# Two query passes for the last batch, deeper expert buffers and other GpSimd costs in an attention and expert kernel

## The chip, the cores and the metric

The kernel runs on one core of a Trainium2 chip. The metric is the device time of one launch in microseconds. The kernel before takes 2341.13 us, the median of 3 runs (2332.34 to 2346.16).

## The reference

The input is 4 batches of 2048 tokens with 256 features. The layer has two halves, each wrapped in a layer norm before and a layer norm after, with a residual:

```python
x = x + layernorm(attention(layernorm(x)))
x = x + layernorm(ffn(layernorm(x)))
```

The attention has 16 heads of 16 features. Queries and keys are projected to one number per token and head, `zq` and `zk`, and a key counts by how near its number is to the query's:

```python
out[i] = sum_j max(0, 1 - abs(zq[i] - zk[j]) / bandwidth[h]) * v[j] / T      # T = 2048
```

The reference computes this with a sort and prefix sums; the value is that of the sum over all 2048 x 2048 pairs of a head. The second half is a mixture of experts: softmax over 64 experts, the best 8 of each token with their weights normalised, at most 128 tokens for an expert (counted in the order of all 8192 tokens, the rest are dropped), each expert a gated layer 256 to 128 to 256, and a shared expert 256 to 512 to 256 that every token passes, scaled by a sigmoid gate:

```python
w, idx = top_k(softmax(x @ gate_w), 8);  w = w / w.sum()
pos = running count of the token within its expert       # pos >= 128: dropped
y = sum over kept (token, expert): w * (silu(g) * u) @ down[e]
out = y + (silu(G) * U) @ shared_down * sigmoid(x @ shared_gate_w)
```

Everything is float32.

## The kernel before

**The loop.** The attention is 1024 units, 256 for each batch: two groups of 8 heads (`NG`), two halves of a group (`p`), 16 tiles of 128 keys (`NT`), 4 heads (`j`). In a unit all 2048 queries of a head (`qb`, broadcast to 128 partitions by `load_q`) meet 128 keys. `score(t)` makes the weights: `abs(q - k)` of 128x2048, mostly on ACT (L1558, Abs with the key as bias), and on DVE in two instructions (L1553, L1555) when the counter `spare` has saved up enough DVE time; then DVE's min and subtract (L1562). `product(t)` multiplies with the values: four matmuls (L1588) of 512 queries on 32 columns of PE, one for each query chunk c, and chunk c is that of the unit c earlier, so the four matmuls of a step have four heads `j` and lie on four column tiles. The sums stay in four PSUM banks (`pa0` to `pa3`) over a group and are brought out by `evict` (L1572), then stored in `cx_d`. The weights live in 13 big tiles of 128x2048 (`NBIG`), and smaller work in 10 slots (`NSLOT`).

**The background.** After each unit `bg.step()` lets the class `Background` issue other work from one list in order of priority. A task has an engine, a cost in units, dependencies, buffers that it takes (`get`) and gives back (`put`), and an optional `lat`, from which the wait of its successors is worked out. `CAP` limits the cost per engine and step, and a task is issued when its dependencies are old enough and its buffers free. Nothing else sets the order in which the engines receive this work. `flush(tasks)` issues the named tasks and all that they depend on at once, and `drain()` empties the list after the loop, with one unit of cost per step. GpSimd's gathers were entered at cost 1.3 and its scatters at 1.9, both with `lat=5`.

The background work of batch b is `prepare(b)` (norm and projections, one batch ahead), and `finish(b)`, put in the list eight units into the next batch: `front(c)` for each of 4 chunks of 512 tokens (transposes, residual, norm, router logits L543), `tail()` (softmax, best 8, codes of the chosen experts transposed into `scT`), `first` (rounds of MAX8 and MATCH_REPLACE, L713 and L715, which choose the earliest tokens of each expert), and `shared(c)`, the shared expert (L573, L587, L589, L602, L607, store to `y_d` at L619, collected in `stored[b]`). For batches 0 and 1 it then enters `all_experts`: 64 experts, each with a load of weights on SP, a gather of up to 128 rows on POOL (L1041), transposes and matmuls (L1047, L1051, L1061), Silu and products, and a scatter with addition to `y_d` (L1066). Four row sets and four weight halves allow for some overlap; expert e waits for the scatter of e-4, its weights for the gather of e-2.

**The tail.** After the loop `bg.flush(tabs + chain)` issues what routing work is left, and the last batch follows: `front_last` (all four chunks), eight rounds of `first`, `merge` and `ranking`, and 15 items, which serve the experts' places that are still free for tokens of batches 2 and 3 (gather L1217, matmuls, two scatters L1258 where an item holds two experts). A scatter waits for `stored[2]`, the shared expert of batch 2. The rest of the list, among it the shared expert of batch 2, goes between `front_last` with its merging and the items:

```python
mine = bg.q
bg.q = mine + rest
ys = stored[2]
```

Then come `shared_last` (the shared expert of the last batch, L911 to L931, kept on chip), and `final` for 16 chunks of 512 tokens (load of `y_d` L1281, add L1288, statistics L1292, power on POOL L1298, norm L1307, an accumulating DMA to the output on POOL L1321). Those of batches 2 and 3 wait for the last item's scatter. A branch for overflowing experts follows and is not taken here.

Of the kernel before, what the change touches and what calls it, by code (L numbers as in the profile page):

```python
# [25 lines left out]
class Background:  # L26
# [8 lines left out]
    def __init__(self, make):  # L35
        self.make = make
        self.free = {}
        self.q = []
        self.t = 0
        self.debt = dict.fromkeys(self.CAP, 0.0)  # L40
        self.spent = dict.fromkeys(self.CAP, 0.0)
        self.alone = False
# [27 lines left out]
    def emit(self, k):  # L70
        for key, r in k.get.items():
            tag, _ = self.free[r].pop(0)
            k.env[key] = self.make(tag)
            k.env["tag", key] = (r, tag)
# [66 lines left out]
def sandwich_kernel(ctx: ExitStack, tc: tile.TileContext, x_in, wqT, bq, wkT, bk, wvT, bv, wprojT, log_bw,  # L141
                    gate_w, sgate_w, sgu_w, sd_w, egu_w, ed_w, out):
    nc = tc.nc
# [36 lines left out]
    cx_d = [dram.tile([NG, P, T], F32, name=f"cx_d{b}") for b in range(B - 1)]  # L180
# [5 lines left out]
    ysh_d = dram.tile([T, F], F32, name="ysh_d")  # L186
# [28 lines left out]
    NS = NT // 2 * P  # L215
    scT = const.tile([P, NS + CAP], F32, name="scT")
# [9 lines left out]
    with ExitStack() as ph:  # L226
# [30 lines left out]
        NES, ess = 4, []  # L257
        bg = Background(make)
        bg.free["slot"] = [(f"s{i}", 0) for i in range(NSLOT)]
# [196 lines left out]
        def finish(b, after=()):  # L456
# [5 lines left out]
            xfree = []  # L462
            def front(c):
# [93 lines left out]
                a = bg.add("act", 0.25, gate, [a])  # L557
                gts = bg.add("dve", 0.1, lambda gt=gt: nc.vector.tensor_scalar(gt, gt, 0.5, 0.5, ALU.mult, ALU.add), [a])
                ready[c] = (done, gt, gts)

            def shared(c):
# [32 lines left out]
                for i2 in range(2):  # L594
# [15 lines left out]
                    if i2 == 0:  # L610
# [8 lines left out]
                free_ys = bg.add("sp", 1.0, lambda ys=ys, r0=r0: nc.sync.dma_start(yrows(r0, CH, 0),  # L619
                                                                                   chunkview(env[ys])),  # L620
                                 yy, put=[] if b == NE else [ys], env=env)
                stored[b].append(free_ys)
                if b == NE:
                    bg.add("sp", 1.0, lambda ys=ys, c=c: nc.sync.dma_start(rows(ysh_d, c * CT, CH), chunkview(env[ys])),
                           [free_ys], put=[ys], env=env)

            def tail():


                lgv = lambda: env["lg"].rearrange("p (n e) -> p n e", e=E + 1)[:, :, :E]  # L630
                mkv = lambda: env["lg"][:, :NT * E].rearrange("p (n e) -> p n e", e=E)
                prv = lambda: env["pr"][:, :NT * E].rearrange("p (n e) -> p n e", e=E)
                mx = t8 = ts_ = None
                t0 = b * NT
                wide = lambda a: a.unsqueeze(2).to_broadcast([P, NT, E])

                def most():
                    nonlocal mx, t8, ts_
                    mx = small.tile([P, NT], F32, tag="mx", name=f"mx_{b}")
                    t8 = small.tile([P, NT, TOPK], F32, tag="t8", name=f"t8_{b}")  # L640
                    ts_ = small.tile([P, NT], F32, tag="ts", name=f"ts_{b}")
# [13 lines left out]
                for i in range(0, NT, 4):  # L655
                    a = bg.add("dve", 0.55, lambda i=i: top(i), [a])
                for i in range(0, NT, 4):
                    a = bg.add("dve", 0.78, lambda i=i: rep(i), [a])

                def sums():  # L660
# [6 lines left out]
                tabs.append(bg.add("sp", 1.0, lambda: nc.sync.dma_start(tabrows(b * T, NT)[:, :, F:TW], prv()), [a],  # L667
                                   put=["pr"], env=env))
                a = bg.add("dve", 1.2, lambda: nc.vector.scalar_tensor_tensor(
                    out=mkv(), in0=mkv(), scalar=0.0, in1=wide(code[:, t0:t0 + NT]), op0=ALU.is_lt, op1=ALU.mult), [a])  # L670
                ev = []
                for r in range(NT // 8):
                    pk = ("psc", r)

                    def tr(r=r, pk=pk):
                        for i in range(4):
                            t = r * 8 + 2 * i
                            nc.tensor.transpose(env[pk][:, i * P:(i + 1) * P],
                                                mkv()[:, t:t + 2, :].rearrange("p a e -> p (a e)"), ident)
                    t_ = bg.add("pe", 0.58, tr, [a], get={pk: "bank"}, put=["lg"] if r == NT // 8 - 1 else [], env=env)  # L680
                    ev.append(bg.add("dve", 0.68, lambda r=r, pk=pk: nc.vector.tensor_copy(
                        scT[:, r * BK:(r + 1) * BK], env[pk]), [t_] + chain[-1:], put=[pk], env=env))
                return ev

            for c in range(NCH):
                front(c)
            if b < NE:
                for c in range(NCH):
                    shared(c)
            a = tail()  # L690
            if b < NE - 1:
                a = first(a, CAP, NS + CAP)
                a = bg.add("dve", 0.2, lambda: nc.vector.tensor_copy(scT[:, NS:], codes), [a])
            elif b == NE - 1:
                a = early(first(a, CAP, NS + CAP), stored[0] + stored[1])
            else:
                a = keep(a, 0)
                a = first([a], LP, NS)
                a = bg.add("dve", 0.2, lambda: nc.vector.tensor_copy(scT[:, NS:NS + LP], codes[:, :LP]), [a])
            chain.append(a)  # L700
            if b == NE:
                for c in range(NCH):
                    shared(c)

        def keep(ev, i):
            return bg.add("sp", 1.0, lambda: nc.sync.dma_start(ck_d[i][:, :], scT[:, :NS]), ev)

        def first(ev, n, w):

            a = ev[-1]  # L710
            for r in range(n // 8):
                c8 = codes[:, r * 8:(r + 1) * 8]
                a = bg.add("dve", 1.25, lambda c8=c8: nc.vector.max(out=c8, in_=scT[:, :w]), ev + [a])  # L713
                if r < n // 8 - 1:
                    a = bg.add("dve", 1.25, lambda c8=c8: nc.vector.match_replace(  # L715
                        out=scT[:, :w], in_to_replace=c8, in_values=scT[:, :w], imm_value=0.0), [a])
# [1073 lines left out]
```

## Time and profile before

| | us |
|---|---|
| median of 3 runs | 2341.13 |
| profiled execution | 2339.91 |
| its span | 2338.0 |
| until the loop starts | 76.7 |
| loop, batch 0 / 1 / 2 / 3 | 473.6 / 489.7 / 500.0 / 505.2 |
| tail, to the first item gather | 82.8 |
| tail, to the first scatter | 76.5 |
| tail, to the last scatter | 68.8 |
| tail, to the end | 64.7 |

The profiled execution is the one whose trace is read here; its span is what the trace covers. The granted clock of TensorE had a mean of 0.954. The stretches are cut at the first unit of each batch and at GpSimd's first item gather, first scatter and last scatter. Engines are PE (matmul), PEld (weight load), DVE, ACT, POOL (GpSimd) and SP (DMA issue). A row of the groups reads: line, engine, operation, output<-inputs, shapes, count | busy time and mean ns of one | idle time of the engine just before, with what ended it. A row of a timeline reads: start, duration, engine, line, operation, and in brackets the idle time before it and its releaser.

### The profile page before, as it was taken

Reading aid. Unit: us, or ns where it says so; the run is one execution under the profiler, and the core shown is the slowest. Engines: PE = TensorE matmul, PEld = TensorE weight load, DVE = VectorE, ACT = ScalarE, POOL = GpSimd, SP = SyncE. Lnnn points to the kernel's source line nnn. Section 1 sums busy time; section 2 is a strip of 40 time slices with the busy share of each in tenths; the row PEclk is TensorE's granted clock in tenths of the full one; section 3 lists DMA queues with packets and bytes.
Section 4 is the critical chain, followed back from the end, with each engine's and each line's share of the span. In section 5 each row is a group of like instructions: output and inputs, shape, how many; then the busy total and the mean of one; then the engine's idle time right before and its main releaser. Section 6 shows DMA issues by size and latency. Waiting matters only on the chain. (4 is left out here: it accounts for less than half of the span.)

```text
span 2338.0 us, 32679 instructions
## 1 busy us (share of the span) xinstructions
PE 1952.5 (84%) x12552; PEld 687.2 (29%) x12552; DVE 1996.1 (85%) x3102; ACT 1966.8 (84%) x1269; POOL 490.4 (21%) x339
## 2 busy tenths in 40 slices
PE   7898979888799899677899887878888889987783
PEld 4332323222223222112222222223332223364342
DVE  4799999898999889999989998989999979886335
ACT  2899999898999998999999998989999989742213
POOL 1001010010120000003200003446553234442463
PEclk9999999999999999989999998999999999988897
DMA  4243534427351202142302014465544243355758
GB/s 127 91 133 120 184 103 153 151 88 264 117 162 64 91 19 70 37 147 69 112 19 81 28 54 122 114 186 151 174 121 136 57 134 90 102 177 147 177 124 197
DMA packets 195078, 274.32 MB, mean 117 GB/s; under 512 B 24833, under 2 KB 165505, under 8 KB 194145
## 3 DMA queue, kind: packets, MB, share of 16 engines
q1 hardware_dynamic: 165680, 235.33, 31.2%
q0 software_dynamic: 23824, 31.70, 8.3%
q10 hardware_dynamic: 5408, 5.11, 0.7%
q8 instruction: 101, 1.65, 0.3%
q14 instruction: 65, 0.52, 0.1%
HBM read 189.18 MB, written 82.90 MB: 116 GB/s over the span
## 5 line engine op out<-in xcount | busy, mean ns | idle before, releaser
L1558 ACT ACTIVATE hat<-qb,nk 128x2048 f32<-128x2048 f32 x959 | 1837.3, 1995 | 112.8 <-DMA qb<-zq_d 57.5
L1588 PE MATMUL pa<-hat,v 128*32 128x512 f32 x8192 | 1115.3, 620 | 284.4 <-DVE hat L1562 272.3
L1562 DVE TENSOR_SCALAR hat<-hat 128x2048 f32<-128x2048 f32 x1024 | 1230.3, 1223 | 97.2 <-ACT hat L1558 91.3
L1588 PEld LDWEIGHTS pa<-hat,v 128*32 128x32 f32 x8192 | 186.2, 110 | 900.0 <-DVE hat L1562 652.6
L1066 POOL DMA_INDIRECT y_d<-s,ix x64 | 147.8, 2309 | 286.7 <-DVE s L1064 145.4
L573 PE MATMUL k<-s,sgu 128*128 128x512 f32 x352 | 198.4, 651 | 0.0
L1041 POOL DMA_INDIRECT s<-tab_d,ix x64 | 106.0, 1657 | 327.6 <-DMA qb<-zq_d 259.0
L499 POOL TENSOR_TENSOR rsc<-rsc,mhalf 128x2 f32<-128x2 f32 x24 | 53.4, 2225 | 521.2 <-DVE rsc L498 521.0
L602 PE MATMUL k<-sd,s 128*128 128x256 f32 x384 | 113.7, 428 | 16.9 <-DVE s L589 7.4
L442 PE MATMUL k<-s,s 128*32 128x512 f32 x768 | 102.4, 592 | 0.0
L602 PEld LDWEIGHTS k<-sd,s 128*128 128x128 f32 x384 | 72.2, 205 | 86.4 <-issue 47.8
L573 PEld LDWEIGHTS k<-s,sgu 128*128 128x128 f32 x352 | 54.8, 192 | 136.3 <-issue 121.2
L305 POOL TENSOR_TENSOR rsa<-rsa,mhalf 128x4 f32<-128x4 f32 x16 | 30.8, 1925 | 290.9 <-DVE rsa L304 285.6
L1553 DVE TENSOR_SCALAR hat<-qb,nk 128x2048 f32<-128x2048 f32 x65 | 83.1, 1279 | 0.1
L1555 DVE TENSOR_SCALAR hat<-hat 128x2048 int32<-128x2048 int32 x65 | 79.9, 1229 | 2.2
L350 PE MATMUL k<-h,s 128*128 128x256 f32 x256 | 73.0, 413 | 0.0
L713 DVE MAX8 codes<-scT 128x8 f32<-128x1152 f32 (+2 forms) x48 | 63.4, 1321 | 0.2
L350 PEld LDWEIGHTS k<-h,s 128*128 128x128 f32 x256 | 45.4, 195 | 54.4 <-issue 48.6
L715 DVE MATCH_REPLACE8 scT<-codes,scT 128x1152 f32<-128x1152 f32 (+2 forms) x44 | 57.6, 1310 | 0.0
L607 DVE TENSOR_SCALAR s<-k,gt 128x256 f32<-128x256 f32 x48 | 22.8, 480 | 36.5 <-PE k L602 32.0
L442 PEld LDWEIGHTS k<-s,s 128*32 128x32 f32 x768 | 31.6, 138 | 54.0 <-issue 53.2
L1258 POOL DMA_INDIRECT y_d<-v,ix x28 | 39.9, 1426 | 23.5 <-DMA y_d<-s 7.9
(319 smaller groups left out, 1643.2 us busy)
## 6 DMA issues: line engine op xcount, KB each, us to landing
qb<-zq_d SPq DMA_DIRECT2D x128, 512.0 KB, 5.5
s<-m_d SPq DMA_DIRECT2D x48, 512.0 KB, 4.8
s<-_attn_hidden_states_dram SPq DMA_DIRECT2D x28, 512.0 KB, 5.5
v_d<-h SPq DMA_DIRECT2D x48, 192.0 KB, 2.6
v<-v_d SPq DMA_DIRECT2D x48, 192.0 KB, 2.5
h<-fn_expert_gate_up_w_dram SPq DMA_DIRECT2D x32, 256.0 KB, 3.5
s<-fn_expert_gate_up_w_dram SPq DMA_DIRECT2D x32, 256.0 KB, 2.8
b<-y_d SPq DMA_DIRECT2D x16, 512.0 KB, 9.3
```

Source lines behind the costliest of these rows:

```text
L350: nc.tensor.matmul(env[pk][:, i * F:(i + 1) * F], lhsT=xv[:, k, o:o + P], rhs=wv[:, k, :], start=(k == 0), stop=(k == KF - 1))
L442: nc.tensor.matmul(env[pz][c * CR:(c + 1) * CR, :], lhsT=xv[:, r, :], rhs=env[mp][:, k * 2 * F:(k + 1) * 2 * F], start=(r == 0 and k == 0) ...
L573: nc.tensor.matmul(env[p_], lhsT=sgu[:, k, o:o + P], rhs=featview(env[xT])[:, k, :], start=(k == 0), stop=(k == KF - 1))
L602: nc.tensor.matmul(env[py][:, i * F:(i + 1) * F], lhsT=env[acts[f // 2]][:, o:o + P], rhs=sd[:, f, :], start=(f == 0), stop=(f == NI - 1))
L713: a = bg.add("dve", 1.25, lambda c8=c8: nc.vector.max(out=c8, in_=scT[:, :w]), ev + [a])
L1041: g = bg.add("pool", 1.3, lambda: nc.gpsimd.indirect_dma_start(out=xg(), out_offset=None, in_=tab_d[half][:, :], in_offset=bass.IndirectOf ...
L1066: s = bg.add("pool", 1.9, lambda: nc.gpsimd.indirect_dma_start(out=y_d[half][:, :], out_offset=bass.IndirectOffsetOnAxis(ap=iv(), axis=0), ...
L1553: nc.vector.tensor_scalar(ht, qb[n][0], k, None, ALU.add)
L1555: nc.vector.tensor_scalar(hi, hi, 0x7fffffff, None, ALU.bitwise_and)
L1558: nc.scalar.activation(ht, qb[n][0], AF.Abs, bias=k)
L1562: nc.vector.tensor_scalar(ht, ht, 1.0, 1.0, ALU.min, ALU.subtract)
L1588: nc.tensor.matmul(pa[k, c][32 * j:32 * j + 32, :], lhsT=vt[b, s].rearrange("p a w -> p (a w)")[:, h // 2 * VW + p * D:h // 2 * VW + p * D ...
```

## The change

**Two passes.** The list `QS` splits the queries of the last batch: the first pass takes queries 0 to 1535, the second the last 512, so the loop has 1280 units. In the second pass the four heads of a unit group share one big tile for the queries and one for the weights ("packed"), each with its 512 columns; a unit is then one ACT (or DVE) instruction of 512 columns, one DVE min/subtract of 512, and one matmul. `spare` is counted by width. `bg.step()` runs only in every third unit of the second pass, with other limits, and five big tiles serve as slots there.

**The routing of the last batch.** `finish(3)`, for the three chunks of the first pass, is put in the list eight units into the second pass, with `shared(c)` for those chunks; its result is added to `y_d` by an accumulating DMA on POOL and stored again in `ysh_d`. `front_last` and `shared_last` handle only the last chunk, and the last eight rounds run over 320 columns instead of 1088. The `finish(3)` part of routing comes under the flush after the loop. The rest of the list goes behind the items.

**The experts.** Eight row sets; six weight halves and all eight sets for the first 40 experts, then four halves and four sets. Expert e waits for the scatter of e-8, its weights for the gather of e-3. `all_experts` also waits for the tables of both batches.

**GpSimd in the order.** A gather counts 1.7 instead of 1.3, with `lat=9`; a scatter 2.4 instead of 1.9.

```diff
+        QS = [(b, 0, T) for b in range(B - 1)] + [(B - 1, 0, LC * CT), (B - 1, LC * CT, T - LC * CT)]
+        NB = len(QS)
...
+        packed = lambda t: 4 * width(t) <= T
...
-            hat[t] = take(f"hat_{b}_{h}_{s}")
-            ht = hat[t][0]
+            w = width(t)
+            if not packed(t):
+                hat[t] = take(f"hat_{t // NU}_{h}_{s}")
+            elif j == 0:
+                hat[t] = take(f"hat_{t // NU}_{h}_{s}")
+            else:
+                hat[t] = (hat[t - j][0][:, j * w:], hat[t - j][1])
+            ht = hat[t][0][:, :w]
...
-            if spare[0] >= 1.3:
+            if spare[0] >= 1.3 * sz:
...
-                spare[0] -= 3.6
+                spare[0] -= 3.6 * sz + 0.18 * (1 - sz)
             else:
-                nc.scalar.activation(ht, qb[n][0], AF.Abs, bias=k)
-                spare[0] += 1.9 - 1.17
+                nc.scalar.activation(ht, q, AF.Abs, bias=k)
+                spare[0] += (1.9 - 1.17) * sz + 0.14 * (1 - sz)
...
-                if not 0 <= tt < B * NU:
+                if not 0 <= tt < NB * NU or c >= width(tt) // BK:
                     continue
...
+                if u == 0 and b == B:
+
+                    bg.CAP = dict(bg.CAP, pe=1.05, dve=0.85)
+                    for i in range(5):
+                        bg.free["slot"].append(bg.free["big"].pop(0))
                 if u == 8 and b > 0:
                     finish(b - 1, after=[last[B - 1]["end"]])
...
-                bg.step()
+                if b < B or u % 3 == 2:
+                    bg.step()
...
-            for c in range(NCH):
+            for c in range(LC, NCH):
...
-            if b == NE:
-                for c in range(NCH):
+            if b >= NE:
+                for c in range(n):
                     shared(c)
...
+                if b == B - 1:
+
+                    free_ys = bg.add("pool", 1.5, lambda ys=ys, r0=r0: nc.gpsimd.dma_start(
+                        yrows(r0, CH, 1), chunkview(env[ys]), accum_op=ALU.add), yy)
...
-            late.append(keep(ev, 1))
-            a = first([late[-1]], LP, NS + LP)
+            lo = (NCH - LC) * 2 * P
+            late.append(keep(ev, B - 1 - NE, 0, lo))
+            a = first([late[-1]], LP, 0, lo + LP)
...
-            mine = bg.q
-            bg.q = mine + rest
             ys = stored[2]
...
+            bg.q += rest
             outs = shared_last(env, exps, gates, xts)
...
-        NES, ess = 4, []
+        NES, NEX, ess = 8, 40, []
...
-                ld = bg.add("sp", 1.0, load, a + gs[e - 2:e - 1], get={w: "half"}, env=env)
+                x = "2" if e < nx and e % 2 else ""
+                ld = bg.add("sp", 1.0, load, a + (gs[e - 3:e - 2] if e >= 3 else []), get={w: "half" + x}, env=env)
...
-                g, sc = expert(env, e, half, lambda e=e: ix[:, e:e + 1], a + out[e - 4:e - 3], ld,
+                g, sc = expert(env, e, half, lambda e=e: ix[:, e:e + 1], a + (out[e - 8:e - 7] if e >= 8 else []), ld,
...
-            g = bg.add("pool", 1.3, lambda: nc.gpsimd.indirect_dma_start(
+            g = bg.add("pool", 1.7, lambda: nc.gpsimd.indirect_dma_start(
...
-                in_offset=bass.IndirectOffsetOnAxis(ap=iv(), axis=0)), deps, get=get[0], env=env, lat=5)
+                in_offset=bass.IndirectOffsetOnAxis(ap=iv(), axis=0)), deps, get=get[0], env=env, lat=9)
...
-            s = bg.add("pool", 1.9, lambda: nc.gpsimd.indirect_dma_start(
+            s = bg.add("pool", 2.4, lambda: nc.gpsimd.indirect_dma_start(
```

## The prediction

> **What bounds the kernel now.** I read the page's head first, then the table by stretches (cut at the batch borders and at the turns of the tail), then the groups by shape, then the timelines of single engines.
>
> ```profile
> span 2338.0 us, 32679 instructions
> ...
> PE 1952.5 (84%) x12552; PEld 687.2 (29%) x12552; DVE 1996.1 (85%) x3102; ACT 1966.8 (84%) x1269; POOL 490.4 (21%) x339
> ```
> Three engines stand at 84 to 85%: no single one bounds the whole. So it must be read by stretch. Columns after start:end are length, then PE, PEld, DVE, ACT and POOL busy, granted clock, DMA share, GB/s:
>
> ```profile
> core 0: us, PE busy (x) PEld busy (x) DVE busy (x) ACT busy (x) POOL busy (x), PEclk, DMA share, GB/s
> ...
> 1540.00:2045.20 505.20, 432.04 (x2880) 150.29 (x2879) 456.51 (x665) 471.15 (x303) 218.88 (x118) 0.98 0.46 123
> 2045.20:2128.00 82.80, 65.85 (x255) 44.02 (x255) 73.00 (x261) 27.79 (x50) 25.03 (x33) 0.82 0.44 131
> 2128.00:2204.50 76.50, 56.40 (x191) 35.27 (x192) 30.87 (x129) 22.86 (x48) 25.30 (x21) 0.81 0.84 199
> 2204.50:2273.30 68.80, 58.25 (x267) 29.01 (x264) 23.79 (x73) 9.01 (x23) 50.02 (x38) 1.00 0.61 133
> 2273.30:2338.00 64.70, 28.98 (x89) 18.13 (x87) 33.60 (x104) 21.88 (x44) 20.67 (x16) 0.73 0.88 197
> ```
> Row one is the loop over the fourth batch: ACT, DVE and PE all above 85%. The other four are the tail, 292.8 us: an opening of 82.8 to the first item gather, 76.5 in which no engine is full, 68.8 of scatters, 64.7 of finals. The loop's work is in three groups, ended by different engines:
>
> ```profile
> L1558 ACT ACTIVATE hat<-qb,nk 128x2048 f32<-128x2048 f32 x959 | 1837.3, 1995 | 112.8 <-DMA qb<-zq_d 57.5 <-PE pa L1588 49.6 <-DMA cx_d<-ct 3.1
> L1562 DVE TENSOR_SCALAR hat<-hat 128x2048 f32<-128x2048 f32 x1024 | 1230.3, 1223 | 97.2 <-ACT hat L1558 91.3
> L1588 PE MATMUL pa<-hat,v 128*32 128x512 f32 x8192 | 1115.3, 620 | 284.4 <-DVE hat L1562 272.3 <-DVE ct L1572 6.0 <-DVE mva L303 0.8
> ...
> L587 ACT ACTIVATE s<-k 128x512 f32<-128x512 f32 x45 | 26.3, 584 | 14.2 <-PE k L573 11.2 <-DMA out_dram<-s 3.0
> ```
> The 76.5 us hole is on POOL's timeline: the item gathers are over at 2137, the first scatter comes 67 us later, released by the store of the third batch's shared expert (y_d<-s, L619), which the scatters have in their dependencies as `stored[2]`:
>
> ```profile
> 2135.93 0.95 POOL L1217 DMA_INDIRECT v<-tab_d,ix  x1 [0.30 <-issue]
> ...
> 2204.55 1.65 POOL L1258 DMA_INDIRECT y_d<-v,ix  x1 [7.89 <-DMA y_d<-s]
> 2206.51 1.43 POOL L1258 DMA_INDIRECT y_d<-v,ix  x1 [0.31 <-issue]
> ```
>
> **Part 1, the loop: one batch of 256 wide units becomes 256 units of 1536 and 256 of 512.** Durations below are start to start where one instruction follows another (the rows' means hold a further 0.1 us of overlap). ACT's Abs of 2048: 1.893 us. Its slope, from Exp of 1024 and of 256 (0.964 and 0.323), is 0.834 ns an element, so 1.708 scales and 0.186 is paid per instruction. Hence 1536 costs 1.466 and 512 costs 0.613. DVE's min and subtract (L1562): 1.135 at 2048, by the same split 0.868 and 0.335. PE: a group of up to four 512-column matmuls on different column tiles takes 0.975 to the next full-array matmul, 0.43 a pass, and a group of three takes no less, as they run side by side.
>
> Counts are from the changed order. Pass 1: 244 Abs on ACT x 1.466 = 358, with background 373; DVE 357 and PE 356. Pass 2: 222 Abs x 0.613 = 136, with background 141; DVE 143; PE 159 (a matmul per unit, background every third unit). Before, the batch held 241 x 1.893 = 456 of ACT, 471 with background. Since the engines take turns at being the limit, I sum the busiest of ACT, DVE and PE over stretches of 16 units: fourth batch before 472.7 (measured 505.2, so 33 or 7% is waiting); after, 384.3 in pass 1 and 165.9 in pass 2. With the same 7% they are 411 and 178, and I add 4 and 5 for one more border each (two evictions of 0.68 and a reload of the query tiles; estimate): 415 + 183 = 598, against 505: **+93**. Nothing hides this: all three engines are in it. SP carries the query tiles in 48 loads instead of 32, of the same bytes; ACT waited 11 us for them in the fourth batch, which is inside the 7%. Nearly half of the work added is ACT's fixed part, 256 x 0.186 = 48.
>
> [...] First, the row: ACT at 512 is in the trace as Silu from PSUM, 0.477 from start to start (L587, mean 584). [...] I take 0.613, because it comes from the same instruction at 2048. The choice moves little, PE being the longer at 159: the pass comes to some 176 by the row. [...]
>
> Second, PE in pass 2. A unit there brings one matmul of its own wait instead of four in a group. In the trace a group's second matmul pass and the next group's first overlap when they are on other column tiles (at 313.4 a late single began, and the next group at 313.5 while its second pass ran to 313.8), and turning between narrow and full modes costs something each way, 0.99 for the group and 1.06 for the full matmul, where two passes in one mode take 0.86:
>
> ```profile
> 899.74 1.13 PE L573 MATMUL k<-s,sgu 128*128 128x512 f32 x2
> 900.80 1.07 PE L1588 MATMUL pa<-hat,v 128*32 128x512 f32 x8
> 901.79 1.12 PE L573 MATMUL k<-s,sgu 128*128 128x512 f32 x2
> ```
> [...] By overlap, three units and one full matmul are 0.975 + 1.056 = 2.03 us, and the pass's PE is 159; with every single paying both of its passes (0.86) it is about 300. I take the overlap, the case the trace shows, and keep 300 as an end.
>
> **Part 2, the experts.** Eight row sets and six weight halves, waits on the scatter eight back instead of four. Before, four experts' Silu (of 64) were left to the tail, and 49 fell in the fourth batch; in the changed order 18 fall in the third batch, 46 in pass 1, none later. POOL is 43% busy in the fourth batch (218.9 of 505.2), so the earlier gathers (1.657) and scatters (2.309) fit, and its larger task costs (1.7, 2.4) only space them. The third batch's sum of the busiest rises from 480.3 to 484.6: **+4**. The five SP loads a third of the queue earlier run where DMA share is 0.29. Its ends: four experts' matmuls (about 4 us of PE each by their rows) gone from the tail, which are in PE's tail sum below, and 10 lost if the earlier traffic delays query reloads. What is late next in the loop stays the hat hand-over of ACT, DVE and PE.
>
> **Part 3, the tail.** Before: 82.8 + 76.5 + 68.8 + 64.7 = 292.8. Added ahead: the rest of `finish` for three chunks of the last batch is flushed before the last chunk: by their rows 7 + 16.7 for the front and 12.9 for softmax and codes, then eight selecting rounds, now 832 wide (2.18 each, scaled from this pair of instructions: 2.71 a round at 1088), less the last replace, 16.2: **53**.
>
> ```profile
> 2108.00 1.29 DVE L713 MAX8 codes<-scT 128x8 f32<-128x1088 f32 x1
> ...
> 2110.72 1.29 DVE L713 MAX8 codes<-scT 128x8 f32<-128x1088 f32 x1
> ```
> Then chunk 3 alone through transposes, statistics, norm, logits and softmax (an estimate of 28: the four chunks before took 82.8 less 21.7 of rounds and 16.5 of merging and ranking, 45, and the chain of one is most of it), eight rounds 320 wide (8.2), merging and ranking (16.5): 106 to the first item gather, **+23**. The hole: the third batch's stores are done inside pass 2, so `stored[2]` no longer holds anything: items need some 18 before the first scatter instead of 76.5 (the first gather's transpose ran 7.5 after it; three more hand-overs at 3.5 each, an estimate): **-58**. What is late next is POOL's own order: 28 scatters (1.4 + 0.3) and the gathers between, 68 (before 68.8): 0. New on POOL are three accumulating stores of the last batch's shared chunks, the third ahead of the last six scatters; they wait for 88 matmuls (40 x 0.86 + 48 x 0.43 = 55 us of PE), which the 106 us opening covers; uncovered they would cost up to those 55; I take 0. Finals: eight, as before, one less tile to add for three of them: 58, **-7**. PE's tail work falls from 178 to 111. Together 106 + 18 + 68 + 58 = 250, **-43**.
>
> **Sum.** +93 + 4 - 43 = +54 on the profiled execution's 2339.91 (span 2338.0), 1.2 under the median 2341.13: about **2394**. Own range: pass 1 400 to 435, pass 2 166 to 205, tail 230 to 270: 2365 to 2425.
>
> **The rivals.** (a) Faster: the tail's hole goes in full and the added opening is hidden behind the drain of pass 2. Then the tail is 210 (83 + 18 + 60 + 49: no scatter waits for a gather, finals overlapped), -83; with 4% waiting in the loop (400 + 172, no border price) it grows 67 and the third batch not at all: 2324. It decides once the tail falls by more than the loop grows. For: 76.5 us without a full engine; against: the flush puts 53 us of DVE-ordered work ahead of the last chunk, and 550 of the loop's 598 us is engine time. Chance 0.11; 0.10 more that both meet within 12 us of no change. (b) Slower by far: single matmuls don't overlap, pass 2 becomes PE's at 300 to 320, total about 2520; the 313.4 instance speaks against, lone waits per matmul for. Chance 0.05. (c) The deeper expert buffers do nothing, since gathers waited for qb<-zq_d 259 of 328 idle us: inside the main case. Main case and its slower neighbours: 0.74 and 0.05.
>
> **The numbers.** About 0.5% (12 us) is what a measurement can tell from no change. Faster 0.11 (a), same 0.10, slower 0.79. The range 2335 to 2450 leaves out most of (a) and (b).
>
> **Right or wrong.** The profile after should show ACT's Abs at 512 near 0.6 start to start, at 1536 near 1.47; pass 1 near 415, pass 2 near 183; from the loop's end to the first item gather about 106; first scatter some 18 later, released by a DVE row and no longer by y_d<-s; scatters at POOL's pace. Pass 2 over 240 means no overlap on PE; a tail under 225 with a loop under +75 makes me wrong on the sign.

## The result and the profile after

| | before | after |
|---|---|---|
| median, us | 2342.12 (4 runs) | 2442.24 (4 runs, 2432.27 to 2450.61) |
| profiled execution, us | 2339.91 | 2450.61 |
| its span, us | 2338.0 | 2448.8 |

The ratio of the times is 1.0432, with a 95% interval of 1.038 to 1.0484: 100 us slower, where 54 were forecast. The median lies inside the outer range of the prediction (2335 to 2450) and 17 us above its own narrower one (2365 to 2425). The profiled execution is the slowest of its four runs, so its trace is 111 us longer than that of before. The head of the page of the kernel after:

```profile
span 2448.8 us, 33205 instructions
...
PE 2038.3 (83%) x12552; PEld 694.6 (28%) x12552; DVE 2036.1 (83%) x3454; ACT 1997.1 (82%) x1465; POOL 462.8 (19%) x336
```

The shares are a little lower than before, so the longer time is not only more work: there is more waiting too. Where it is shows in the table by stretches of the kernel after (third batch, first pass, second pass; then the tail to the first item gather, to the first scatter, to the last scatter, to the end; columns as in the prediction):

```profile
1044.40:1546.40 502.00, 427.27 (x2663) 130.38 (x2663) 457.82 (x654) 477.53 (x287) 104.51 (x56) 0.98 0.32 92
1546.40:2008.40 462.00, 409.29 (x2287) 143.69 (x2288) 362.19 (x631) 383.26 (x315) 174.47 (x113) 0.96 0.47 119
2008.40:2183.40 175.00, 170.09 (x762) 53.86 (x762) 144.38 (x405) 136.12 (x224) 7.21 (x11) 0.98 0.27 80
2183.40:2284.60 101.20, 59.51 (x193) 37.12 (x194) 83.77 (x310) 29.41 (x51) 25.25 (x28) 0.75 0.54 126
2284.60:2310.00 25.40, 13.60 (x61) 7.52 (x60) 8.43 (x39) 4.47 (x11) 9.17 (x9) 0.87 1.11 284
2310.00:2388.50 78.50, 65.59 (x289) 33.05 (x287) 26.59 (x82) 7.88 (x21) 51.67 (x39) 0.93 0.64 145
2388.50:2448.80 60.30, 0.00 (x0) 0.00 (x0) 27.39 (x97) 16.59 (x32) 22.23 (x17) 0.50 0.93 211
```

Against the prediction, stretch by stretch:

| | before | predicted | after |
|---|---|---|---|
| third batch | 500.0 | 504 | 502.0 |
| fourth batch, or first pass | 505.2 | 415 | 462.0 |
| second pass | | 183 | 175.0 |
| tail to first item gather | 82.8 | 106 | 101.2 |
| to first scatter | 76.5 | 18 | 25.4 |
| to last scatter | 68.8 | 68 | 78.5 |
| to the end | 64.7 | 58 | 60.3 |

One row carries most of the miss: the first pass, 47 us over. The tail is 15 over in all; the rest is small (the part ahead of the third batch, which has no row, is 4 us longer than before). In the second row of the table ACT is busy 383 of 462 us and DVE 362; before, they were busy 471 and 457 of 505. The groups of the kernel after, by shape, say that the instructions are not to blame:

```profile
L1613 ACT ACTIVATE hat<-qb,nk 128x1536 f32<-128x1536 f32 x246 | 367.7, 1565 | 30.0 <-PE pa L1649 15.2 <-DMA qb<-zq_d 12.2 <-DVE hat L1619 2.1
...
L1613 ACT ACTIVATE hat<-qb,nk 128x512 f32<-128x512 f32 x225 | 139.5, 710 | 7.3 <-PE pa L1649 7.3
...
L1619 DVE TENSOR_SCALAR hat<-hat 128x512 f32<-128x512 f32 x256 | 92.4, 420 | 1.3 <-ACT hat L1613 0.2
```

Less the 0.1 us by which the records of neighbours overlap, ACT's Abs takes 1.465 and 0.610 us, where 1.466 and 0.613 were predicted. What ACT waits for ahead of its Abs is small here too (30 us and 7 us). The missing time lies ahead of other instructions. The waits of the first pass in the kernel after (engine, line waited at, releaser: us in total, times, longest):

```profile
ACT s L1091 <- PE k L1084: 51.7, 34, 9.5
...
DVE s L1087 <- PE k L1080: 39.4, 23, 7.7
...
PE k L1080 <- DMA s<-tab_d,ix: 30.3, 10, 7.7
DVE s L1097 <- PE k L1094: 29.8, 32, 1.9
...
PEld k L1080 <- DMA s<-tab_d,ix: 19.8, 7, 7.2
```

These lines are all inside the experts. The transposes of the gathered rows (L1080) wait on PE for the gather, DVE's copy (L1087) waits for the transposes, ACT's Silu (L1091) for the first matmuls, DVE's last product (L1097) for the second. The same three hand-overs in the fourth batch of the kernel before, where no wait of PE for a gather is listed:

```profile
DVE s L1064 <- PE k L1061: 5.7, 9, 1.5
...
DVE s L1054 <- PE k L1047: 5.1, 10, 0.9
...
ACT s L1058 <- PE k L1051: 1.1, 2, 0.9
```

One such place, in the timeline of all engines of the kernel after:

```profile
1673.16 3.03 ACT L1613 ACTIVATE hat<-qb,nk 128x1536 f32<-128x1536 f32 x2
...
1675.70 0.69 PE L1080 MATMUL k<-ident,s 128*128 128x128 f32 x2 [6.30 <-DMA s<-tab_d,ix]
...
1676.42 0.42 DVE L1087 COPY s<-k 128x256 f32<-128x256 f32 x1 [4.94 <-PE k L1080]
...
1682.75 0.28 ACT L1091 ACTIVATE s<-k 128x128 f32<-128x128 f32 x1 [6.57 <-PE k L1084]
```

PE was given the transpose ahead of the next products, so for 6.3 us it does nothing while the transpose waits for its gather. DVE stands behind a copy of that transpose, ACT behind a Silu of 0.28 us that waits 6.57 us. One late gather has stopped all three engines that carry the loop. The gather itself was quick. It was issued late, because it stood on POOL behind a scatter:

```profile
1668.24 1.59 POOL L1099 DMA_INDIRECT y_d<-s,ix  x1 [9.44 <-DVE hat L1619]
1672.82 0.99 POOL L1074 DMA_INDIRECT s<-tab_d,ix  x1 [2.99 <-DMA y_d<-s,ix]
```

POOL waited 9.44 us for DVE and 2.99 us for a scatter's landing; the transpose ran 2.9 us after the gather was issued. Such late gathers are the plainest waits in a timeline, but the experiments show that they are not most of the waiting.

### The profile page after: what moved, and what is told of

Read it like the earlier page. It is cut to its first block, busy times and chain, and to the rows that moved or that the text cites. A ratio compares the mean times of both kernels' runs of the same rounds, so it can differ in the third digit from the quotient of the medians.

```text
span 2448.8 us, 33205 instructions
## 1 busy us (share of the span) xinstructions
PE 2038.3 (83%) x12552; PEld 694.6 (28%) x12552; DVE 2036.1 (83%) x3454; ACT 1997.1 (82%) x1465; POOL 462.8 (19%) x336
## 5 line engine op out<-in xcount | busy, mean ns | idle before, releaser
L1613 ACT ACTIVATE hat<-qb,nk 128x2048 f32<-128x2048 f32 (+2 forms) x1189 | 1881.0, 1661 | 121.2 <-PE pa L1649 58.9
L1649 PE MATMUL pa<-hat,v 128*32 128x512 f32 x8192 | 1198.3, 620 | 234.0 <-DVE hat L1619 222.0
L1619 DVE TENSOR_SCALAR hat<-hat 128x2048 f32<-128x2048 f32 (+2 forms) x1280 | 1251.7, 1008 | 74.0 <-ACT hat L1613 67.7
L581 PE MATMUL k<-s,sgu 128*128 128x512 f32 x436 | 245.4, 648 | 0.0
L1608 DVE TENSOR_SCALAR hat<-qb,nk 128x2048 f32<-128x2048 f32 (+2 forms) x91 | 89.1, 980 | 0.1
L1610 DVE TENSOR_SCALAR hat<-hat 128x2048 int32<-128x2048 int32 (+2 forms) x91 | 84.3, 926 | 3.2
L729 DVE MAX8 codes<-scT 128x8 f32<-128x1152 f32 (+3 forms) x56 | 65.3, 1165 | 0.5
L1091 ACT ACTIVATE s<-k 128x128 f32<-128x128 f32 x64 | 17.4, 273 | 58.7 <-PE k L1084 58.3
L1087 DVE COPY s<-k 128x256 f32<-128x256 f32 x64 | 26.5, 420 | 44.4 <-PE k L1080 44.2
L1097 DVE TENSOR_SCALAR s<-k,s 128x256 f32<-128x256 f32 x64 | 30.8, 482 | 36.5 <-PE k L1094 36.3
L731 DVE MATCH_REPLACE8 scT<-codes,scT 128x1152 f32<-128x1152 f32 (+3 forms) x51 | 59.1, 1160 | 0.0
```

Source lines behind the costliest of these rows:

```text
L581: nc.tensor.matmul(env[p_], lhsT=sgu[:, k, o:o + P], rhs=featview(env[xT])[:, k, :], start=(k == 0), stop=(k == KF - 1))
L729: a = bg.add("dve", cost, lambda c8=c8: nc.vector.max(out=c8, in_=scT[:, lo:hi]), ev + [a])
L1608: nc.vector.tensor_scalar(ht, q, k, None, ALU.add)
L1610: nc.vector.tensor_scalar(hi, hi, 0x7fffffff, None, ALU.bitwise_and)
L1613: nc.scalar.activation(ht, q, AF.Abs, bias=k)
L1619: nc.vector.tensor_scalar(ht, ht, 1.0, 1.0, ALU.min, ALU.subtract)
```

## The experiments

Three theories for the first pass were tried: the experts come too closely; units of 1536 columns leave too little slack whatever the experts do; and, after the first runs, the planner's waits, which are counted in units, are too short in microseconds when units are a quarter shorter. Two theories for the tail were tried with them. Ratios are to runs of the kernel before on the same chip (medians 2335.77 to 2337.76). "Over" below is the stretch's time less its busiest engine's work, summed over stretches of 16 units as in the prediction; both the work and "over" are worked out from the program's order and the durations of the trace of before, so they are estimates. "ACT idle" is measured, the stretch's time less ACT's busy time in that run's own trace. "Behind PE" is the sum of the rows ACT or DVE <- PE k in the waits, and "gathers" PE's wait at the transposes for a gather.

| run | stretch | busiest engine | took | over | ACT idle | behind PE | gathers |
|---|---|---|---|---|---|---|---|
| before | fourth batch | 473 | 505 | 33 | 34 | 16 | 0 |
| experts_only | fourth batch | 473 | 523 | 50 | 55 | 55 | 11 |
| before_noexperts | fourth batch | 458 | 487 | 29 | 41 | 22 |  |
| after | first pass | 384 | 462 | 78 | 79 | 132 | 30 |
| passes_only | first pass | 405 | 448 | 43 | 61 | 93 | 0 |
| after_paced | first pass | 360 | 422 | 62 | 60 | 114 | 4 |
| after_noexperts | first pass | 387 | 406 | 20 | 39 | 46 |  |
| after_steps | first pass | 361 | 399 | 38 | 37 | 41 | 6 |
| after_lags | first pass | 364 | 404 | 40 | 38 | 41 | 18 |
| after_caps | first pass | 379 | 439 | 61 | 62 | 101 | 10 |

The two measures agree within 5 us but for passes_only and the two runs without experts, where the estimate of "over" is lower by 12 to 19 us. Differences of that size between these three runs and the others are not to be relied on.

**The experts' part undone (passes_only).**

```diff
-        NES, NEX, ess = 8, 40, []
+        NES, ess = 4, []
...
-                ld = bg.add("sp", 1.0, load, a + (gs[e - 3:e - 2] if e >= 3 else []), get={w: "half" + x}, env=env)
+                ld = bg.add("sp", 1.0, load, a + gs[e - 2:e - 1], get={w: "half"}, env=env)
```

> The changed kernel with the experts' part undone: four row sets, four weight halves, the old waits (scatter of e-4, gather of e-2) and GpSimd's old costs; the two passes stay. Theory A (in the first pass the experts run too closely for GpSimd, 4.4 in 16 units of 1.5 us, their gathers arrive late, and PE, which takes its work in order, holds the products back): the four row sets hold the experts at about 3 in 16 units, so the first pass falls from 462 us to about 415 to 425, and the median from 2442 to about 2395 to 2405. Theory B (units of 1536 columns leave too little slack between the engines, whatever the experts do): the first pass stays at 450 to 465, the median at 2430 to 2445.

The median was 2441.80 us, ratio 1.0451 (1.0414 to 1.0487): no better than the whole change. The first pass took 448.1 us, between the two theories, and it held more work than that of the change. By either measure it waited more than the kernel before (43 over against 33, ACT idle 61 against 34), so the experts' part is not needed for a slow first pass. What did go with it are the late gathers: PE's wait for them fell from 30.3 us to nothing. DVE and ACT still stood 93 us behind PE.

**The experts' part alone (experts_only).** The reverse edit, on the kernel before.

> The kernel before with the experts' part alone: eight row sets, six weight halves, the new waits and costs; one pass for the last batch. Theory A: the same crowding appears in the fourth batch, but its units last 1.97 us, so GpSimd keeps up better; the fourth batch 505 us before becomes 505 to 530, and the median 2341 becomes 2335 to 2370. Theory B: nothing in the loop is held up by the experts, fourth batch 495 to 505, median 2325 to 2345.

The median was 2348.81 us, ratio 1.006 (1.0031 to 1.0088). The fourth batch took 523 us, 18 more at the same work, and the tail 283 for 293. All of it is waiting, by either measure, and 11 us of PE's wait for gathers is new.

**The experts slowed (after_paced).**

```diff
+                if u == 0 and b == B - 1:
+                    bg.CAP = dict(bg.CAP, pool=0.8)
```

> The changed kernel with the planner's limit for GpSimd set from 1.5 to 0.8 in the first pass (it stays there in the second), so that an expert comes every 5 units; all buffers as changed. Theory A: the first pass falls from 462 to about 415 to 425 as with the undone experts. Theory B, and a theory that the deeper buffers themselves hold up the loop: it stays at 450 to 465. Some of the third batch's shared expert moves behind the loop with it (69 of its and the last batch's 512-wide matmuls against 40), so the tail gets longer by 20 to 40 us and the median says less than the first pass.

The first pass took 422.5 us, as the first theory said; but the table shows that much of this was because 24 us of work had left it. Over is still 62, with gathers all but in time (3.8 us), and the median 2454.49 us, ratio 1.051 (1.0482 to 1.0538). The pace of the experts explains a part at most. The tail took 317 us, 52 more than in the change where 20 to 40 were expected. With work leaving a stretch, the stretch's time alone tells nothing; over does.

**Without the experts (after_noexperts, before_noexperts).**

```diff
-            for e in range(E):
+            for e in range(0):
```

> The changed kernel without the 64 experts of the first two batches (their loads, gathers, matmuls and scatters are left out). The busiest engine's work in the first pass sums to 387 us. If the experts make the waiting of the first pass, it takes 395 to 410; if narrow units do it alone, 425 to 445.

> The kernel before without the same 64 experts. The busiest engine's work in the fourth batch sums to 458 us. If the experts make the waiting, it takes 465 to 475; if the loop waits of itself, about 485 to 492, the 33 us of waiting seen with experts.

The first pass took 406.2 us, as it should if the experts make the waiting, and the fourth batch 486.7, as it should if the loop waits of itself (one execution each; 2319.27 and 2263.13 us in all). So narrow units wait no more than wide ones when there are no experts, 20 us against 29 (ACT idle 39 against 41). With the experts it is 78 against 33. It takes both: the experts, and the short unit.

**Fewer steps (after_steps).**

```diff
-                if b < B or u % 3 == 2:
+                if b < B - 1 or (b == B - 1 and u % 4 != 3) or (b == B and u % 3 == 2):
                     bg.step()
```

> The changed kernel with background steps in three of every four units of the first pass, so that a step there stands for as much time as in the wide batches. The busiest engine's work over stretches of 16 units sums to 361 us in the first pass (384 in the changed kernel, which took 462; 360 in the paced one, which took 422). Theory C (the planner counts waits and engine limits in units; at 1536 columns a unit is a quarter shorter, so PE is given too much and what ACT and DVE take from it comes late, and they stand in order behind it): the first pass falls to 380 to 395. Theory D (the experts' deep buffers hold up the loop whatever the step): 415 to 430. The work put off comes back behind the loop (68 wide shared-expert matmuls against 40), so the median stays within 25 us of the changed kernel's in either case.

The first pass took 398.8 us with almost as many experts in it (48 scatters against 49), and over fell from 78 to 38. It is 4 us above the range that was given and far under the other one. The median was 2423.48 us, ratio 1.038 (1.0358 to 1.0401), some 19 under the change. The waits of its first pass, at the same places:

```profile
DVE s L1097 <- PE k L1094: 20.2, 16, 5.2
...
DVE s L1087 <- PE k L1080: 10.9, 12, 2.2
...
ACT s L1091 <- PE k L1084: 7.4, 7, 2.0
...
PE k L1080 <- DMA s<-tab_d,ix: 5.7, 2, 5.3
```

ACT's wait at the Silu went from 51.7 to 7.4 us. But fewer steps change two things, the waits and the load per unit. The next two runs take them apart.

**The waits alone (after_lags), the load alone (after_caps).**

```diff
+            v = self.LAG.get((d.eng, k.eng), 0) + d.late if d.lat is None else (d.lat + 3) // 2
+            return v + self.more if v else v
...
+                if u == 0 and b >= B - 1:
+                    bg.more = int(b == B - 1)
```

> The changed kernel with the planner's waits between dependent tasks of different engines one unit longer in the first pass (those of zero units stay); its limits per unit as in the changed kernel. The busiest engine's work in the first pass sums to 364 us. If the waits, too short in time for units a quarter shorter, are the cause, the first pass takes 395 to 410 (a surplus of 30 to 45 as with fewer steps); if it is the load per unit, 425 to 440 (60 to 75).

```diff
+                if u == 0 and b == B - 1:
+                    bg.CAP = {e: 0.75 * c for e, c in bg.CAP.items()}
```

> The changed kernel with all of the planner's limits per unit times 0.75 in the first pass, its waits as in the changed kernel. The busiest engine's work in the first pass sums to 379 us. If the load per unit is the cause, the first pass takes 410 to 420; if the waits are, 440 to 455.

With waits one unit longer the first pass took 403.8 us and 40 over, inside the range given, and the median was 2427.68 us, ratio 1.0396 (1.0376 to 1.0417). With lower limits it took 439.2 us and 61 over, a hair under the range for the other cause, and the median was 2444.47, ratio 1.0478 (1.0444 to 1.0513). So the waits carry most of it: less work in the pass does not explain it, since after_paced had as little (360 against 364) and was 62 over. The waits of the first pass with one unit more:

```profile
PE k L1082 <- DMA s<-tab_d,ix: 17.6, 4, 7.3
ACT s L1093 <- PE k L1086: 13.9, 13, 4.0
DVE s L1099 <- PE k L1096: 12.5, 15, 2.3
DVE s L1089 <- PE k L1082: 12.2, 7, 5.6
...
PEld k L1082 <- DMA s<-tab_d,ix: 11.0, 2, 5.5
```

The three hand-overs fell from 121 us to 39, PE's wait for gathers from 30 to 18. The experiment lengthened every wait of that kind at once, so it does not say which one mattered. One unit more is also more than the quarter that was lost (a wait of one unit from PE to DVE became two), and no run tried it in wide units, so it is not shown that only the shortening was at fault.

Little of the gain reaches the median. The first pass is 63 us shorter with fewer steps and 58 with longer waits, but the medians are only 19 and 15 under the change (12 and 8 by the ratios, whose intervals overlap with the change's). Background work is put off instead: the tails take 314 and 318 us, not 265.

**The tail (shared_apart, shared_apart_behind).** Both are the kernel before with the third batch's shared expert kept in a table of its own, which its finals load and add; the second also puts the rest of the list behind the items.

```diff
-            ys = stored[2]
+            ys = []
...
-                        final(env, c, deps, tag=tag)
+                        f = final(env, c, deps, lambda k=k: env[k][:, :CH * F], [ld], tag)
```

> The kernel before with one thing changed in the tail: the third batch's shared expert is not stored where the item scatters add, but only in its own table, which the finals of that batch load and add; so the scatters wait for no store. One pass, experts as before. Theory of the tail (its 76.5 us between the first item gather and the first scatter are that wait, and PE's 178 us of tail work fit beside the rest): the hole shrinks to 15 to 30 us, the tail goes from 293 to 235 to 260, the median to 2285 to 2310. Rival (PE's own work in the tail is the limit and the wait only shows where it is felt): the tail stays at 275 to 295, the median at 2325 to 2345.

> The kernel before with the third batch's shared expert kept apart, as in the earlier run, and with the rest of the list put behind the items instead of ahead of them, as the change does. If the order of the tail's work keeps the scatters (the shared expert's matmuls stand ahead of the items on PE and DVE), the first scatter comes 20 to 35 us after the first gather instead of 63, and the tail falls from 296 us to 255 to 280, the median to 2300 to 2325. If the amount of work and of transfers in the tail sets its end, the hole moves behind the scatters and the median stays at 2330 to 2345.

The medians were 2339.54 us, ratio 1.0011 (0.9998 to 1.0024), and 2336.08 us, ratio 1.0007 (0.9994 to 1.0019): no change, twice, as the rival in each expectation had it. Without the wait for the store, the first scatter still came 63 us after the first gather. On POOL in shared_apart:

```profile
2133.39 0.95 POOL L1213 DMA_INDIRECT v<-tab_d,ix  x1 [0.30 <-DMA b<-fn_expert_gate_up_w_dram]
...
2189.06 1.64 POOL L1254 DMA_INDIRECT y_d<-v,ix  x1 [7.61 <-DVE v L1250]
```

Its releaser is now the item's own last product on DVE. With the items ahead of the rest the scatters did start early, 23.6 us after the first gather, but then the tail's end was what the rest made of it (shared_apart_behind: to the first scatter, to the last, to the end):

```profile
2124.60:2148.20 23.60, 17.18 (x83) 12.21 (x83) 13.07 (x59) 6.35 (x16) 11.02 (x9) 0.92 0.97 290
2148.20:2242.00 93.80, 66.15 (x284) 32.55 (x281) 35.68 (x137) 19.57 (x45) 66.08 (x50) 0.89 0.81 179
2242.00:2333.30 91.30, 59.33 (x177) 34.62 (x175) 43.14 (x115) 26.69 (x54) 21.62 (x16) 0.83 0.69 160
```

In the last 91.3 us PE is busy 59 us; in the change it is busy 0 in its last 60.3. The hole was closed by the order, and the tail still took 291 us: its idle time had been moved, not filled. What shortens the tail is work taken out of it: without the experts the kernel before has all of the third batch's shared expert inside the loop (and no experts left over), and its tail is 254 us instead of 293.

**More of that work in the loop, one pass (before_limits, before_limits_2).** The first raises the limits in the fourth batch, the second from the third batch on.

```diff
+                if u == 0 and b == B - 1:
+                    bg.CAP = dict(bg.CAP, pe=1.3, dve=1.0, act=0.5)
```

> The kernel before with higher limits in the fourth batch (PE 1.3, DVE 1.0, ACT 0.5 per unit instead of 0.88, 0.75, 0.4), nothing else. Four experts and 16 wide and 18 narrow shared-expert matmuls move from the tail into the fourth batch (its busiest engine's work 483 us instead of 473). If work in the tail counts fully and in the loop less, the fourth batch takes 515 to 525 (505) and the tail 265 to 275 (293), median 2325 to 2340. If crowding the loop costs more than it frees, the fourth batch takes 530 or more and the median is 2340 to 2365.

> The kernel before with the higher limits (PE 1.3, DVE 1.0, ACT 0.5) from the third batch on; nothing else. In its order 18 experts fall in the third batch (11 before), 46 in the fourth, none in the tail, and 16 wide and 18 narrow matmuls of the third batch's shared expert are left to the tail (32 and 48 before). If the loop has room for work of the tail and its waits are long enough in wide units: third batch 503 to 512, fourth 512 to 524, tail 252 to 264, median 2318 to 2334. If crowding eats the gain: loop longer by 30 or more, median 2335 to 2350.

The first gave 2333.46 us, ratio 0.9978 (0.9963 to 0.9994): the fourth batch took 523 us (18 more), the tail 262 (30 less). It is the only version with all the work that is clear of the kernel before, by 0.2%. The second gave 2353.94 us, ratio 1.007 (1.0046 to 1.0095): the third batch took 516.8, the fourth 542.4, the tail 251, so the loop lost 54 us where the tail gained 41; the median is above both ranges given. Its fourth batch took 19 us more than the first's at the same limits and the same estimated work (482 and 483). DVE and ACT stood 86 us behind PE there, against 49, so it is the same kind of waiting; why there was more of it was not settled.

## Why the prediction was right, and where it was off

**Bound and sign: right.** All three engines bound the loop, nothing hid the second pass, and the loop grew by more than the tail fell. The size was not right: 100 us against 54, in the main because one term was too small. The two kernels without the experts stand at 2263 and 2319 us, +56, but that this is close to the +54 of the sum is partly luck: in them the last batch grew by 82 us instead of 93 and the tail fell by 32 instead of 43.

**Instruction costs: right.** ACT by the split of the 2048 row, 0.613 us at 512 columns, where 0.610 was measured; the row taken from PSUM, 0.477, would have been wrong. The rival of a PE that can't overlap its single matmuls fell: pass two took 175 us, not 300. Three units and a full matmul repeat every 2.05 us on PE in the kernel after, 2.03 predicted, and a group of three takes 0.99 of it, as a group of four did before:

```profile
2056.86 1.12 PE L581 MATMUL k<-s,sgu 128*128 128x512 f32 x2
2057.92 1.06 PE L1649 MATMUL pa<-hat,v 128*32 128x512 f32 x6
2058.91 1.12 PE L581 MATMUL k<-s,sgu 128*128 128x512 f32 x2
```

Two readings behind the prediction do not stand. At 313.4 us, the place named for an overlap, PE is idle in the trace of before (from 313.1 to 313.9); a case of the kind lies at 303.0, where a single matmul starts and three of the next group follow at 303.1, ahead of its second pass at 303.4. And the 259 us for which the gathers waited are one wait, that of POOL ahead of the first gather, so they say nothing of how the later ones run.

**The mis-sized term: "with the same 7%".** The working took the fourth batch's waiting as a share of its work and carried it over to the first pass. There it was 20%: 78 of 384. The runs show that it goes with the planner's steps instead: fewer steps, or one unit more of waiting, brought it to 38 and 40, and without the experts there was as little (20, and ACT idle 39 us against 79). The planner holds a task back a number of units, and a unit went from 1.97 us to between 1.5 (384 over 256) and 1.80 (462 over 256). Four units from PE to ACT were 7.9 us and became 6.0 to 7.2; ACT's wait at the Silu went from 1.1 us to 51.7. The gathers are another matter. The change gave what follows them six units instead of four (`lat=9` against 5), so their time did not get shorter, and their median landing was 3.5 us against 4.0. Where one was late in the row above, POOL had issued it late, and none was late without the experts' part (passes_only). In the second pass, where a step comes every third unit, the 7% was even too much (9 us over in 175). The step ratio was in the diff, for the second pass and not for the first, and it was priced only as load.

Mending the waits does not bring back the forecast: the median falls by at most 15 to 19 of the 46 us that were missed, since work moves to the tail. How much the first pass could gain with the same work in it stays open.

**Part 2, "+4 for the experts": wrong by its place.** In the third batch it was +2. In the pass it was set against the whole row of waits, and was given nothing. Alone it costs 18 us in the fourth batch and 12 in the median (2348.81 against 2337.24). Beside the two passes, undoing it changed nothing in the sum: the first pass got 14 us shorter, the tail 10 longer (275 against 265). PE's late gathers belong to this part: 30 us with it and none without, 11 in wide units. Of the experts' part, GpSimd's costs in the order were not tried on their own, and how much of the 78 us is due to the deeper buffers stays open (43 without the whole part, or 61 by ACT's idle time).

**The tail: -27 instead of -43, with the wrong cause for its main term.** The hole did close (25.4 us), but its wait for the store was not what made the tail long. shared_apart took that wait away and kept the hole; shared_apart_behind closed the hole by the order, as the change does, and kept the tail's length. What these runs leave as the cause of a shorter tail is work. PE's work in the tail was to fall from 178 to 111 us by the prediction's sum; PE's busy time in the traces fell from 209 to 139. Of it, 48 us are the third batch's shared expert (32 wide matmuls of 0.86 and 48 of 0.43), which the change does inside the loop. The stretch from the first scatter to the last took 78.5 us instead of 68. POOL waited there 11 us for scatters to land, where it waited 4 before, and one of the three accumulating stores that the change puts in its queue stands among them, in the kernel after:

```profile
2371.74 1.40 POOL L629 DMA_DIRECT2D y_d<-s  x1 [2.25 <-DMA y_d<-v,ix]
2373.45 1.51 POOL L1290 DMA_INDIRECT y_d<-v,ix  x1 [0.30 <-DVE v L1286]
2378.65 1.41 POOL L1290 DMA_INDIRECT y_d<-v,ix  x1 [3.69 <-DMA y_d<-v,ix]
```

These stores were predicted as free since the shared work behind them would be ready. This one waited for no shared work, but 2.25 us for a scatter to land, and then took 1.40 us itself. The longer wait of the scatter after it, 3.69 us, is again for a scatter by the profile; whether the store lengthened it was not tried.

## What to carry to other kernels

When an order counts its waits in loop steps, a shorter step shortens every wait; here DVE and ACT, which took their work in order, then stood at the background's late results (121 us at three hand-overs of the first pass, against 12 in the fourth batch before). Scale the steps or the waits with the step's length, and do it before judging the split. When the last releaser of a hole is a store, ask what made the store late: if it is a list of work, taking the wait away can leave the hole or move it, as in the two runs that tried it (tails of 296 and 291 us against 293), and what shortened the tail here was taking work out of it (262 us in before_limits). When a stretch is mended by putting work off, look at where that work lands before counting the gain. To compare a stretch between versions that hold different work, subtract the busiest engine's work first, and check that estimate against a measured idle time.

## What the runs showed of the hardware

Not expected: in one place a transpose at the head of PE's order waited for a gather, and PE, DVE and ACT stood for 6.30, 4.94 and 6.57 us, though the transpose ran 2.9 us after the gather was issued; the delay was POOL's, 9.44 us of it for DVE, in front of a scatter that stood ahead of the gather. In the tail an accumulating store waited 2.25 us for a scatter into the same table to land. And the 25.4 us from the first item gather to the first scatter are the fullest of the stretches shown for the kernel after, 284 GB/s at a DMA share of 1.11, at a time when PE, DVE and ACT are each busy less than 14 us.
